# The end of an audio-tower kernel: the last token group transposed by VectorE and SBUF moves instead of TensorE, routed by sums, its expert weights gathered in three pieces

## The chip, the core and the metric

The kernel runs on one core of a Trainium2 chip. The metric is the device time of one execution in microseconds (us); of several executions the median is taken. All data is float32.

## The reference

64 clips of 80,000 samples are cut into 157 frames of 512 samples, and each frame is turned into 512 DCT coefficients. Then comes one layer of a causal phase-memory attention with a gate, and after it a feed-forward part with one expert for each clip:

```python
h = _L0_tok_ref(x)                         # (64, 157, 512)
h = h + _L0_attn_ref(_layernorm(h), ...)
y = _layernorm(h)
scores = softmax(mean(y, axis=1) @ Wg + bg)       # (64, 16)
idx = argmax(scores); gate = scores[idx]
h = h + gate * (y @ We[idx] + be[idx])            # We: (16, 512, 512)
```

The change concerns this last part for the last four clips: the mean over a clip's tokens, the choice of its expert, the fetch of that expert's 512x512 matrix, and the product of the 157 tokens with it.

## The kernel before, in words

The 64 clips go in 16 groups (`NG`) of four (`GB`). A clip's 157 tokens are padded to 160 and cut into five tiles of 32 tokens; a tile of 128 partitions holds 32 tokens of each of the four clips. Tile number 4 (`TAIL`) has only 29 real tokens for each clip. The tiles are worked in the order `ORDER` = 4, 0, 1, 2, 3.

The order of all instructions on every engine is the order of the calls in the text of the kernel (`manual_schedule`); each engine takes its own in order. SyncE, ScalarE and GpSimd also issue DMAs, in the same order as their other work; a DMA that reuses a semaphore waits for the earlier one on it. PSUM is a pool of four buffers (`psum`) of two banks, given out in turn; a buffer is free again when its last reader is done.

The stages of neighbouring groups overlap. While group g goes through values, gate and attention, group g-1 is routed, its expert weights are gathered, and its expert products are done at the end of g's stages. So after the attention of the last group (g = 15) the five expert products of group 14 and the whole expert part of group 15 remain. That end is the place of the change. In the numbering of the kernel before it runs as follows.

- **Normalise.** `statistics2` (line 756) takes mean and variance of a tile on VectorE, the reciprocal deviation and the shift on GpSimd (`deviation`, `shifts`, lines 237 to 244). `normal2` (772) makes the normalised tile x2 (128 tokens x 512) on ScalarE (line 784), or, where `at_end` (768) says so, on VectorE (782) without the shift.
- **Turn.** The expert product needs x2 with features on the partitions. For groups 0 to 14 `turn_blocks` (787) transposes 32x32 blocks on VectorE (line 793), and `move_blocks` (795) brings the blocks to their partitions with 16 DMAs within SBUF (line 805). For the last group `turn_x2` (809) uses four TensorE transposes for each tile (line 816) and a copy out of PSUM (817).
- **Route.** Groups 0 to 14 sum the turned tokens on VectorE (`xsum`, 820) and multiply by the router's weights there (`route_own`, lines 837 to 841), then one matmul (848) adds over partitions and spreads the result. The last group multiplies all tokens by the router's weights on TensorE (`route_tokens`, line 858), sums on VectorE (`route_sum`, 865) and spreads by a matmul (`route_spread`, 871). `pick` (878 to 891) then finds logits, maximum and expert number on VectorE.
- **Fetch.** `fetch` (893) computes row numbers on VectorE (903) and gathers each clip's matrix by an indirect DMA of GpSimd (907). The last group's four matrices go to buffers no longer used (`wv`, `wg`, `spare`, `t_v`), in two pieces each; between the two pieces `biases` (called at 905) runs `pick_gate` (the softmax value, with one exponential on ScalarE, line 920) and `bias`, which gathers the experts' bias rows (937). The bias buffer `be` is single.
- **Product.** `expert_chunk` (949) is four matmuls in four 32-column groups of TensorE, one for each clip, for one of four parts c of the 512 features (line 953); four chunks make a tile. `add_bias` (944, line 947) adds the gated bias to the residual, `expert_out` (961, line 964) adds the gated product, both on VectorE, and stores the tile (line 971). A tile of the last two groups goes out by SyncE, ScalarE or GpSimd as lines 968 to 970 say.

In the trace a float32 matmul shows as two records, so a chunk of four matmuls has eight. The end, word for word:

```python
    expert(g - 1, ORDER[0])
    normal2(g, 1)
    turn_x2(g, TAIL)
    ...
    add_bias(g - 1, ORDER[1])
    expert(g - 1, ORDER[1], routes)
    ...
    for c in range(2):
        for n, ps in zip(order, banks):
            expert_chunk(g, n, c, ps)
```

`routes` puts `route_tokens` ahead of chunk 1 of that tile, and the spread, the pick and the fetch ahead of chunk 2. The last group's five tiles first do chunks 0 and 1 of all tiles, which need the first pieces of the weights alone, and then chunks 2 and 3 tile by tile.

Of the kernel before, what the change touches and what calls it, by code (L numbers as in the profile page):

```python
# [14 lines left out]
F32 = mybir.dt.float32  # L15
# [38 lines left out]
def audio_tower(ctx: ExitStack, tc: tile.TileContext, a, out):  # L54
# [118 lines left out]
    rowbase = load("rowbase", [P, 3])  # L173

    wv = const.tile([P, C, D], F32, name="wv", tag="wv")
    wg = const.tile([P, C, D], F32, name="wg", tag="wg")
# [543 lines left out]
    def output_product(g, i):  # L720

        s = S[g]
        ps = product(g, i, fac_o)
        (r11, r12), (r21, r22) = ([r[:, :, n : n + H] for n in (0, H)] for r in s["res2"])
        last = g + 1 == NG
        more = lambda to, x: add(to, to, x)
        if i == 1:
            s["u"] = [p2.tile([P, 2, H], F32, tag="u", name="u") for _ in range(2)]
            nc.scalar.copy(s["u"][0], ps)
        first, second = s["u"]  # L730
        if i == 2:
            add(r11, ps, r11)
            if last:
                add_bias(g - 1, ORDER[0])
        elif i == 6:
            add(first, ps, first)
            more(r12, first)
            more(r21, first)
        elif i == 7:
            add(second, ps, first)  # L740
            more(r22, second)
        elif i == 5:
            add(r22, ps, r22)
        elif i == 3:
            add(r12, ps, r12)
        elif i == 4:
            add(r21, ps, r21)
            for of in ((2,), (3,)) if last else ((2, 3),):
                statistics2(g, of)

    def output_tail(g):
        s = S[g]
# [14 lines left out]

    def at_end(g, n):

        return g + 1 == NG and n in (3, 0, 1)  # L770

    def normal2(g, n):
        s = S[g]
# [13 lines left out]
    def turn_blocks(g, n):  # L787

        s = S[g]
        if n == TAIL:  # L790
            s["blocks2"] = p1.tile([P, C * GB, LP], F32, tag="gT", name="turned2")
        to = s["blocks2"].rearrange("p (q c) t -> p c q t", c=C)[..., Q * n : Q * (n + 1)]
        nc.vector.transpose(to, s.pop(("x2", n)).rearrange("p (c q t) -> p c q t", c=C, q=GB))

    def move_blocks(g):

# [12 lines left out]
    def turn_x2(g, n, copy=nc.scalar.copy):  # L809
        s = S[g]  # L810
        if n == TAIL:
            x = p1.tile([P, C, 2 * HN], F32, tag="xT", name="x2T_last", bufs=2)
            s["x2T"] = x.rearrange("p c (b t) -> p c b t", b=GB)
        x, tr = s.pop(("x2", n)), bank()
        for c in range(C):
            nc.tensor.transpose(tr[:, c * P : (c + 1) * P], x[:, c * P : (c + 1) * P], ident)
        copy(s["x2T"][:, :, :, Q * n : Q * (n + 1)], tr.rearrange("p (c b t) -> p c b t", c=C, b=GB))


    def xsum(g, lo, hi):  # L820

# [29 lines left out]
    def route_tokens(g):  # L851

        s = S[g]
        s["each"] = ps = bank()[:, :L]
        rwg = s.pop("rwg")
        for c in range(C):
            for b in range(GB):
                nc.tensor.matmul(
                    ps[Q * b : Q * (b + 1), :], rwg[:, c, :], s["x2T"][:, c, b, :L], start=(c == 0), stop=(c == C - 1)
                )  # L860

    def route_sum(g):
        s = S[g]
        s["tot"] = tot = p2.tile([P, 1], F32, tag="tot", name="tot")
        nc.vector.tensor_reduce(tot, s.pop("each"), AX.X, ALU.add)

    def route_spread(g):

        s = S[g]
        ps = bank()[:, :P]  # L870
        nc.tensor.matmul(ps, s.pop("tot").to_broadcast([P, P]), ident, start=True, stop=True)
        s["all"] = ps.rearrange("p (b e) -> p b e", b=GB)[:, :, :E], 1.0 / L

    t = lambda name, shape, dt=F32: p2.tile(shape, dt, tag=name, name=name)
    wide = [P, GB, E]
# [14 lines left out]
        s["rev"] = rev = t("rev", [P, GB])  # L890
        nc.vector.tensor_reduce(rev, score, AX.X, ALU.max)

    def fetch(g, rooms=(), parts=1, between=lambda: None):
        s = S[g]
        ws = [
            rooms[b] if b < len(rooms) else p1.tile([P, C * D], F32, tag="we", name="we", bufs=GB) for b in range(GB)
        ]
        n = C * D // parts
        of = a["we"].rearrange("r (k n) -> (r k) n", k=parts)
        for k in range(parts):  # L900
            rows = t("rows", [P, GB], I32)
            base = rowbase[:, parts + k - 1 : parts + k]
            nc.vector.tensor_scalar(rows, s["rev"], float(-P * parts), base, ALU.mult, ALU.add)  # L903
            if k:
                between()
            for b in range(GB):
                nc.gpsimd.indirect_dma_start(  # L907
                    out=ws[b][:, n * k : n * (k + 1)],
                    out_offset=None,
                    in_=of,  # L910
                    in_offset=bass.IndirectOffsetOnAxis(ap=rows[:, b : b + 1], axis=0),
                )
        s["ws"] = [w.rearrange("p (c o) -> p c o", c=C) for w in ws]

# [46 lines left out]
    def expert_out(g, n, ps):  # L961
        s = S[g]
        o, at = s["res"][n], Q * BLOCK[n]
        nc.vector.scalar_tensor_tensor(o, ps, s["gate"], o, ALU.mult, ALU.add)
        for i in range(GB):

            for lo, hi in ((0, Q),) if n < TAIL else ((0, Q // 2), (Q // 2, LT)):
                queue = nc.sync if g + 1 < NG or i % 2 == 0 else nc.scalar
                if g + 2 == NG and n in ORDER[1:4]:
                    queue = nc.gpsimd  # L970
                queue.dma_start(out=out[GB * g + i, at + lo : at + hi, :], in_=o[Q * i + lo : Q * i + hi, :])

    def expert(g, n, between=lambda c: None):
# [287 lines left out]
        attention(g)  # L1261

    g = NG - 1
    expert(g - 1, ORDER[0])
    normal2(g, 1)
    turn_x2(g, TAIL)
    turn_x2(g, 2)
    turn_x2(g, 3, nc.vector.tensor_copy)
    turn_x2(g, 0)
    turn_x2(g, 1, nc.vector.tensor_copy)  # L1270


# [4 lines left out]
    def biases():  # L1277
        pick_gate(g)
        bias(g)

    def routes(c):
        if c == 1:
            route_tokens(g)
            route_sum(g)
        elif c == 2:
            route_spread(g)
            pick(g)
            fetch(g, [*flat, all_v.rearrange("p i c o -> p (i c o)")], 2, biases)

    add_bias(g - 1, ORDER[1])  # L1290
    expert(g - 1, ORDER[1], routes)
    add_bias(g - 1, ORDER[2])
    expert(g - 1, ORDER[2])
    for n in (3, 4):
        add_bias(g - 1, ORDER[n])
        expert(g - 1, ORDER[n])

    last = psum()
    banks = [last[:, 0, :], *(bank() for _ in range(3)), last[:, 1, :]]
# [6 lines left out]
    for n, ps in zip(order, banks):  # L1306
        for c in range(2, C):
            expert_chunk(g, n, c, ps)
        expert_out(g, n, ps)
# [3 lines left out]
def _constants():  # L1313
# [15 lines left out]
    def trig(half, n, turn):  # L1329
# [10 lines left out]
    setsel = np.tile(np.repeat(np.eye(SETS), PLANES, axis=0), (2, 1))  # L1340
    f = lambda x: np.ascontiguousarray(x, dtype=np.float32)

    sums = [x.sum(axis=0) for x in tables]
    table_sums = np.concatenate([sums[0] + sums[1], sums[2] + sums[3], sums[4], sums[5]]) / -D
    return {
# [11 lines left out]
        "rowbase": f(np.stack([n * (np.arange(P) + P * E) + k for n, k in ((1, 0), (2, 0), (2, 1))], axis=1)),  # L1357
    }


# [61 lines left out]
```

## Time and profile before

| what | value |
|---|---|
| median of 3 runs (lowest, highest) | 1303.95 us (1301.6, 1304.43) |
| the profiled execution's own time | 1301.98 us |
| its span (first to last instruction or landing) | 1300.0 us |
| TensorE busy | 1293.2 us, 99% |
| VectorE busy | 1023.6 us, 79% |
| GpSimd busy | 592.7 us, 46% |
| ScalarE busy | 431.9 us, 33% |
| granted TensorE clock, mean | 0.999 |
| DMA moved | 144.46 MB, mean 111 GB/s |

How to read it: durations of the profile are those of the one profiled execution. TensorE's matmuls overlap, so its busy time is not a measure of how well it is used, and a gap in it shows only as a fall below 100%. The queries used in what follows can be limited to a window of time, given in us from the start of the span.

### The profile page before, as it was taken

To read this page: it belongs to the slowest core of one execution; us is meant where nothing else is said; L and a number is where in the kernel's file an instruction comes from. 1 tells how busy PE (TensorE), PEld (TensorE's weight loads), DVE (VectorE), ACT (ScalarE), POOL (GpSimd) and SP (SyncE) were. 2 spreads that over 40 slices of the span, in tenths; PEclk is the share of its full clock that TensorE was granted. 3 is DMA by queue.
4 is the path that set the end of the run, shared out by engine and by line. 5 is a ranking of instruction groups with operands and counts; after the bars stand their busy time and mean duration, and the time that the engine had idled before them with its cause. 6 is when DMAs were issued, how large, how long until landed. Compare 5 with 4: busy or idle time off the path is not lost.

```text
span 1300.0 us, 26072 instructions
## 1 busy us (share of the span) xinstructions
PE 1293.2 (99%) x10152; PEld 864.7 (67%) x10152; DVE 1023.6 (79%) x2056; ACT 431.9 (33%) x768; POOL 592.7 (46%) x781
## 2 busy tenths in 40 slices
PE   9999999999999999999999999999999999999998
PEld 5677666676666767666676666766666676666762
DVE  6888787878877887788878878788778877888583
ACT  2525334142432324334242331424323243342410
POOL 2356445344553446435444453446434454354424
PEclk9999999999999999999999999999999999999999
DMA  7015224252442425323252342424323262241506
GB/s 242 1 52 178 76 61 173 61 171 75 114 147 54 152 75 177 93 57 146 80 183 76 77 174 49 166 75 131 128 64 145 75 193 77 58 154 36 181 9 210
DMA packets 60578, 144.46 MB, mean 111 GB/s; under 512 B 14136, under 2 KB 31432, under 8 KB 52520
## 3 DMA queue, kind: packets, MB, share of 16 engines
q1 hardware_dynamic: 45620, 62.68, 17.6%
q0 software_dynamic: 14336, 79.47, 17.2%
q8 instruction: 81, 1.33, 0.4%
q10 hardware_dynamic: 500, 0.64, 0.2%
q14 instruction: 41, 0.34, 0.1%
HBM read 102.47 MB, written 20.62 MB: 95 GB/s over the span
## 4 chain that ended last, share of the span: by engine, by line
PE 97%; DMA 1%; POOL 1%; issue 0%; SPq 0%; DVE 0%; POOLq 0%
PE mm L445 29%; PE mm L953 20%; PE mm L658 17%; PE mm L250 10%; PE mm L705 9%; PE mm L270 3%; PE mm L272 3%; PE mm L601 3%; PE mm L637 1%; PE mm L689 1%; DMA tables<-in_table_sums 1%; DMA t_v<-in_we,rows 1%; PE mm L201 0%; PE mm L219 0%; PE mm L684 0%
## 5 line engine op out<-in xcount | busy, mean ns | idle before, releaser
L953 PE MATMUL mm<-we,x2T 128*32 128x512 f32 x2400 | 263.8, 593 | 0.0
L953 PEld LDWEIGHTS mm<-we,x2T 128*32 128x32 f32 x2400 | 75.0, 110 | 165.6 <-issue 165.5
L237 POOL TENSOR_SCALAR rstd<-mv 128x2 f32<-128x2 f32 (+1 forms) x50 | 11.7, 235 | 241.0 <-DVE mv L233 240.9
L516 POOL TENSOR_TENSOR v<-v,bv 128x512 f32<-128x512 f32 (+1 forms) x45 | 72.7, 1632 | 101.2 <-ACT v L465 101.2
L705 PE MATMUL mm<-att,v 32*128 32x320 f32 (+3 forms) x2048 | 113.2, 357 | 0.0
L705 PEld LDWEIGHTS mm<-att,v 32*128 32x128 f32 x2048 | 94.6, 185 | 22.0 <-issue 12.6
L784 ACT ACTIVATE x<-res,shift,rstd 128x512 f32<-128x512 f32 x61 | 46.4, 807 | 172.7 <-POOL shift L244 171.9
L327 POOL TENSOR_TENSOR res<-res,bo 128x512 f32<-128x512 f32 x64 | 95.7, 1514 | 13.1 <-ACT res L323 13.0
L100 DVE TENSOR_TENSOR gT<-mm,gT 128x320 f32<-128x320 f32 (+3 forms) x128 | 71.2, 566 | 31.7 <-PE mm L658 28.7
L712 DVE TENSOR_TENSOR gT<-mm,gT 128x320 f32<-128x320 f32 x128 | 59.5, 485 | 42.4 <-PE mm L705 42.3
L237 POOL TENSOR_SCALAR dev<-mv 128x5 f32<-128x5 f32 (+1 forms) x20 | 4.9, 244 | 188.7 <-DVE mv L233 188.1
L232 DVE BATCH_NORM_STATS2 st<-res 128x6 f32<-128x512 f32 x128 | 87.9, 686 | 3.3
L445 PE MATMUL mm<-t_o,sum 128*128 128x256 f32 x384 | 85.5, 379 | 0.0
L445 PE MATMUL mm<-t_v,sum 128*128 128x256 f32 x360 | 80.1, 379 | 0.0
L445 PEld LDWEIGHTS mm<-t_o,sum 128*128 128x128 f32 x384 | 73.0, 190 | 9.9
L676 ACT ACTIVATE gT<-gT,hbg 128x320 f32<-128x320 f32 (+1 forms) x90 | 45.6, 554 | 100.1 <-DVE gT L100 100.1
L323 ACT ACTIVATE res<-res,shift,more 128x512 f32<-128x512 f32 x64 | 46.9, 803 | 87.2 <-POOL more L313 87.2
L907 POOL DMA_INDIRECT we<-in_we,rows x60 | 59.9, 998 | 34.4 <-DVE rows L903 20.4
L445 PEld LDWEIGHTS mm<-t_v,sum 128*128 128x128 f32 x360 | 68.4, 190 | 9.3
L250 PE MATMUL mm<-wv,xT 128*128 128x512 f32 x160 | 71.8, 592 | 0.0
L658 PE MATMUL mm<-sum,wg 128*128 128x320 f32 (+1 forms) x240 | 69.2, 431 | 0.0
L658 PE MATMUL mm<-xT,wg 128*128 128x317 f32 x240 | 68.9, 430 | 0.0
(223 smaller groups left out, 2832.3 us busy)
## 6 DMA issues: line engine op xcount, KB each, us to landing
xT<-in_frames SPq DMA_DIRECT2D x32, 640.0 KB
out<-res SPq DMA_DIRECT2D x236, 64.0 KB
x2T<-turned SPq DMA_DIRECT2D x150, 80.0 KB
x2T<-turned POOLq DMA_DIRECT2D x90, 80.0 KB, 1.9
scale<-row SPq DMA_DIRECT2D x15, 320.0 KB
out<-res_t SPq DMA_DIRECT2D x62, 32.0 KB
out<-res_t SPq DMA_DIRECT2D x62, 26.0 KB
wg<-in_wg SPq DMA_DIRECT2D x1, 1024.0 KB
```

What stands on the lines that cost most here:

```text
L100: add = lambda *x: nc.vector.tensor_tensor(*x, ALU.add)
L232: nc.vector.bn_stats(st, h)
L250: nc.tensor.matmul(ps, tile_of(x[:, c], n), w[:, c, :], start=(c == 0), stop=(c == C - 1))
L323: nc.scalar.activation(s["res"][n], s["res"][n], AF.Identity, bias=shift, scale=more)
L327: nc.gpsimd.tensor_tensor(r, r, bo, ALU.add)
L445: nc.tensor.matmul(ps[:, b, :], lhs[:, c, P * b : P * (b + 1)], w[:, c, :], start=(first and c == 0), stop=(c == 1), skip_group_check=not ...
L516: nc.gpsimd.tensor_tensor(v, v, by, ALU.add)
L658: nc.tensor.matmul(ps[:, o, :width], w[:, c, o * P : (o + 1) * P], rhs[:, c, :width], start=(first and c == 0), stop=(c == 1), skip_group_ ...
L705: nc.tensor.matmul(to, s["v", n][q, c * P : (c + 1) * P], by, start=(n == 3), stop=(n == TAIL))
L712: nc.vector.tensor_tensor(th, r[:, :, 0], th, ALU.mult)
L907: nc.gpsimd.indirect_dma_start(out=ws[b][:, n * k : n * (k + 1)], out_offset=None, in_=of, in_offset=bass.IndirectOffsetOnAxis(ap=rows[:, ...
L953: nc.tensor.matmul(ps[Q * i : Q * (i + 1), :], s["x2T"][:, c, i, Q * n : Q * (n + 1)], s["ws"][i][:, c, :], start=(c == 0), stop=(c == C - 1),
```

## The change

In words:

- The last group's x2 tiles are transposed by `turn_blocks` on VectorE, and `move_last` moves the blocks by 16 DMAs of 32 partitions x 640 elements, eight issued by SyncE and eight by ScalarE. `turn_x2` goes.
- `route_tokens` now reads x2 before it is turned: for each tile, each of four feature parts and each of four 32-column groups one matmul with 32 stationary columns and a moving operand of four columns, which hold ones for the tokens of each clip. That is 80 matmuls. `route_features` multiplies the sums by the router's weights and reduces, on VectorE; `route_spread` is four matmuls with 64 moving columns.
- The sums stand between the second and third chunk of group 14's second expert tile, the spread, the pick and the fetch ahead of the first chunk of its third tile. The outputs of group 14's first two tiles are written after the fetch is issued; its bias adds come in one go.
- `fetch` for the last group has three pieces of each matrix: a quarter, a quarter, and a half. All row numbers are computed first. The gather of the bias rows stands after all of them.
- The last group's bias adds come one at a time, each ahead of the tile's output.
- Statistics of tiles 2 and 3 of the last group are taken together as for other groups, and only tile 1 is normalised on VectorE.
- The stores of three tiles of group 14 (12 DMAs) go by ScalarE instead of GpSimd. The constant `rowbase` grows from 3 to 12 columns.

The diff, cut to its core:

```diff
-            for of in ((2,), (3,)) if last else ((2, 3),):
-                statistics2(g, of)
+            statistics2(g, (2, 3))
...
-        return g + 1 == NG and n in (3, 0, 1)
+        return g + 1 == NG and n == 1
...
+    def move_last(g):
+        s = S[g]
+        x = p1.tile([P, GB, C, LP], F32, tag="xT", name="x2T_last", bufs=2)
+        of = s["blocks2"].rearrange("p (q c) t -> p q c t", c=C)
+        for b in range(GB):
+            for q in range(GB):
+                queue = nc.sync if q % 2 == 0 else nc.scalar
+                queue.dma_start(out=x[Q * q : Q * (q + 1), b], in_=of[Q * b : Q * (b + 1), q])
+        s["x2T"] = x.rearrange("p b c t -> p c b t")
...
+    def route_tokens(g, of):
+        s = S[g]
+        if "sums2" not in s:
+            s["sums2"] = psum()
+        for n in of:
+            x = s["x2", n]
+            at = 4 + GB * (n == TAIL)
+            for c in range(C):
+                for q in range(GB):
+                    nc.tensor.matmul(
+                        s["sums2"][Q * q : Q * (q + 1), 0, GB * c : GB * (c + 1)],
+                        x[:, c * P + Q * q : c * P + Q * (q + 1)],
+                        rowbase[:, at : at + GB],
+                        start=(n == TAIL and c == 0),
+                        stop=(n == 1),
+                        skip_group_check=True,
+                    )
+
+    def route_features(g):
+        s = S[g]
+        total = s["sums2"][:, 0, : C * GB].rearrange("p (c b) -> p b c", c=C)
+        by = s.pop("rwg")[:, :, :E].rearrange("p c e -> p e c")
+        part = p2.tile([P, GB, E, C], F32, tag="u", name="part")
+        over = [P, GB, E, C]
+        nc.vector.tensor_tensor(part, by.unsqueeze(1).to_broadcast(over), total.unsqueeze(2).to_broadcast(over), ALU.mult)
+        own = p2.tile([P, GB * E], F32, tag="own", name="own")
+        nc.vector.tensor_reduce(own, part.rearrange("p b e c -> p (b e) c"), AX.X, ALU.add)
+        s["own"] = own
 
     def route_spread(g):
         s = S[g]
-        ps = bank()[:, :P]
-        nc.tensor.matmul(ps, s.pop("tot").to_broadcast([P, P]), ident, start=True, stop=True)
+        own, ps = s.pop("own"), s.pop("sums2")[:, 1, : GB * E]
+        for q in range(GB):
+            rows = slice(Q * q, Q * (q + 1))
+            nc.tensor.matmul(ps[rows], mean[:, rows], own, start=True, stop=True)
...
+    def fetch(g, rooms=()):
+        s = S[g]
+        ws = rooms or [p1.tile([P, C * D], F32, tag="we", name="we", bufs=GB) for b in range(GB)]
+        pieces = ((4, 0), (4, 1), (2, 1)) if rooms else ((1, 0),)
...
+        for i, (parts, k) in enumerate(pieces):
+            base = rowbase[:, i + len(rooms) // GB : i + len(rooms) // GB + 1]
+            nc.vector.tensor_scalar(rows[:, i], s["rev"], float(-P * parts), base, ALU.mult, ALU.add)
+        for i, (parts, k) in enumerate(pieces):
+            n = C * D // parts
+            of = a["we"].rearrange("r (k n) -> (r k) n", k=parts)
             for b in range(GB):
                 nc.gpsimd.indirect_dma_start(
                     out=ws[b][:, n * k : n * (k + 1)],
...
                 if g + 2 == NG and n in ORDER[1:4]:
-                    queue = nc.gpsimd
+                    queue = nc.scalar
...
     g = NG - 1
-    expert(g - 1, ORDER[0])
+    first = psum()[:, 0, :]
+    for c in range(C):
+        expert_chunk(g - 1, ORDER[0], c, first)
+    for n in (TAIL, 2, 3):
+        turn_blocks(g, n)
     normal2(g, 1)
-    turn_x2(g, TAIL)
-    turn_x2(g, 2)
-    turn_x2(g, 3, nc.vector.tensor_copy)
-    turn_x2(g, 0)
-    turn_x2(g, 1, nc.vector.tensor_copy)
+    turn_blocks(g, 0)
...
+    def sums(c):
+        if c == 2:
+            route_tokens(g, (TAIL, 2, 3, 0, 1))
+            route_features(g)
+            turn_blocks(g, 1)
+            move_last(g)
 
     def routes(c):
-        if c == 1:
-            route_tokens(g)
-            route_sum(g)
-        elif c == 2:
+        if c == 0:
             route_spread(g)
             pick(g)
-            fetch(g, [*flat, all_v.rearrange("p i c o -> p (i c o)")], 2, biases)
+            fetch(g, [*flat, all_v.rearrange("p i c o -> p (i c o)")])
+            expert_out(g - 1, ORDER[0], first)
+            pick_gate(g)
+            add_bias(g - 1, ORDER[1])
+            expert_out(g - 1, ORDER[1], second)
+            for n in ORDER[2:]:
+                add_bias(g - 1, n)
+            bias(g)
 
+    second = psum()[:, 0, :]
+    for c in range(C):
+        sums(c)
+        expert_chunk(g - 1, ORDER[1], c, second)
+    expert(g - 1, ORDER[2], routes)
+    for n in ORDER[3:]:
+        expert(g - 1, n)
...
-    for n in order:
-        add_bias(g, n)
     for n, ps in zip(order, banks):
+        add_bias(g, n)
         for c in range(2, C):
             expert_chunk(g, n, c, ps)
         expert_out(g, n, ps)
```

More of the change, by code (lines that the diff above doesn't have):

```diff
@@ L172, in audio_tower @@
     revexp = load("revexp", [P, GB, E])
-    rowbase = load("rowbase", [P, 3])
+    rowbase = load("rowbase", [P, 4 + 2 * GB])
     wv = const.tile([P, C, D], F32, name="wv", tag="wv")
@@ L792, in turn_blocks @@
         to = s["blocks2"].rearrange("p (q c) t -> p c q t", c=C)[..., Q * n : Q * (n + 1)]
-        nc.vector.transpose(to, s.pop(("x2", n)).rearrange("p (c q t) -> p c q t", c=C, q=GB))
+        nc.vector.transpose(to, s["x2", n].rearrange("p (c q t) -> p c q t", c=C, q=GB))
+    def move_last(g):
[7 more added lines that the diff above has]
+        s["x2T"] = x.rearrange("p b c t -> p c b t")
     def move_blocks(g):
@@ L807, in move_blocks @@
         yield
[L809 to L817, printed above, removed]
     def xsum(g, lo, hi):
@@ L849, in route_all @@
         s["all"] = ps.rearrange("p (b e) -> p b e", b=GB), D / L
-    def route_tokens(g):
+    def route_tokens(g, of):
         s = S[g]
[L854 to L862, printed above, removed]
-        s = S[g]
-        s["tot"] = tot = p2.tile([P, 1], F32, tag="tot", name="tot")
-        nc.vector.tensor_reduce(tot, s.pop("each"), AX.X, ALU.add)
+        if "sums2" not in s:
[13 more added lines that the diff above has]
+                    )
@@ L867, in route_spread @@
     def route_spread(g):
         s = S[g]
-        ps = bank()[:, :P]
-        nc.tensor.matmul(ps, s.pop("tot").to_broadcast([P, P]), ident, start=True, stop=True)
-        s["all"] = ps.rearrange("p (b e) -> p b e", b=GB)[:, :, :E], 1.0 / L
+        own, ps = s.pop("own"), s.pop("sums2")[:, 1, : GB * E]
+        for q in range(GB):
+            rows = slice(Q * q, Q * (q + 1))
+            nc.tensor.matmul(ps[rows], mean[:, rows], own, start=True, stop=True)
+        s["all"] = ps.rearrange("p (b e) -> p b e", b=GB), D / L
@@ L891, in pick @@
         nc.vector.tensor_reduce(rev, score, AX.X, ALU.max)
-    def fetch(g, rooms=(), parts=1, between=lambda: None):
+    def fetch(g, rooms=()):
         s = S[g]
[L895 to L905, printed above, removed]
+        ws = rooms or [p1.tile([P, C * D], F32, tag="we", name="we", bufs=GB) for b in range(GB)]
+        pieces = ((4, 0), (4, 1), (2, 1)) if rooms else ((1, 0),)
+        rows = [
+            p2.tile([P, len(pieces), GB], I32, tag="each", name="rows")
+            if rooms
+            else t("rows", [P, GB], I32).unsqueeze(1)
+        ][0]
+        for i, (parts, k) in enumerate(pieces):
[4 more added lines that the diff above has]
+            of = a["we"].rearrange("r (k n) -> (r k) n", k=parts)
             for b in range(GB):
@@ L910, in fetch @@
                     in_=of,
-                    in_offset=bass.IndirectOffsetOnAxis(ap=rows[:, b : b + 1], axis=0),
+                    in_offset=bass.IndirectOffsetOnAxis(ap=rows[:, i, b : b + 1], axis=0),
                 )
@@ L1275, in audio_tower @@
     flat[2] = flat[2][:, : C * D]
-    def biases():
-        pick_gate(g)
-        bias(g)
+    def sums(c):
[4 more added lines that the diff above has]
+            move_last(g)
     def routes(c):
-        if c == 1:
-            route_tokens(g)
-            route_sum(g)
-        elif c == 2:
+        if c == 0:
             route_spread(g)
             pick(g)
-            fetch(g, [*flat, all_v.rearrange("p i c o -> p (i c o)")], 2, biases)
[L1290 to L1296, printed above, removed]
+            fetch(g, [*flat, all_v.rearrange("p i c o -> p (i c o)")])
[13 more added lines that the diff above has]
+        expert(g - 1, n)
     last = psum()
@@ L1303, in audio_tower @@
             expert_chunk(g, n, c, ps)
-    for n in order:
+    for n, ps in zip(order, banks):
         add_bias(g, n)
-    for n, ps in zip(order, banks):
         for c in range(2, C):
@@ L1341, in _constants @@
     f = lambda x: np.ascontiguousarray(x, dtype=np.float32)
+    bases = np.stack([n * (np.arange(P) + P * E) + k for n, k in ((1, 0), (4, 0), (4, 1), (2, 1))], axis=1)
+    member = np.kron(np.eye(GB), np.ones((Q, 1)))
     sums = [x.sum(axis=0) for x in tables]
@@ L1356, in _constants @@
         "revexp": f(np.tile(E - np.arange(E), (P, GB, 1))),
-        "rowbase": f(np.stack([n * (np.arange(P) + P * E) + k for n, k in ((1, 0), (2, 0), (2, 1))], axis=1)),
+        "rowbase": f(np.concatenate([bases, member, member * (np.arange(P)[:, None] % Q < LT)], axis=1)),
     }
```

## The prediction

> **What bounds the kernel now.** The page says TensorE (PE) is busy for 99% of the span, so I looked for the one stretch where it isn't: the last 46 us. The chain of waits, read from 1254 us on, shows what that stretch is made of (columns: start, duration, what ran or what was waited for).
>
> ```profile
> 1254.26 3.57 PE mm L953 x32
> 1257.83 2.40 PE mm L816 x20
> 1260.23 0.99 PE mm L953 x8
> 1261.22 1.11 PE mm L858 x32
> 1262.33 0.86 PE mm L953 x8
> 1263.19 0.42 PE mm L871 x2
> 1263.61 1.90 PE mm L953 x16
> ...
> 1265.95 1.08 POOL wv L907
> ...
> 1271.18 2.67 issue
> ...
> 1279.37 7.29 DMA t_v<-in_we,rows
> 1286.66 0.04 issue
> 1286.71 8.79 PE mm L953 x74
> ```
>
> After 1265.95 the chain leaves PE. It runs through GpSimd's (POOL's) nine gathers, and the landing of the last (t_v, second half) lets PE finish. From 1286.71 everything is fixed: 8.8 us of matmuls, one VectorE (DVE) pass of 0.75, the last stores until 1300.0. So **the end is the landing of the last gathered weights plus 13.3 us**; what PE saves earlier counts only through that. The wait timeline of GpSimd says why the gathers take so long:
>
> ```profile
> 1274.08 0.95 POOL L937 DMA_INDIRECT be<-in_be,expi  x1 [2.89 <-DVE res L947]
> 1275.33 0.94 POOL L907 DMA_INDIRECT wv<-in_we,rows  x1 [0.30 <-issue]
> ```
>
> The bias gather stood 2.9 us in the middle of the queue, waiting for the old bias's last reader. In three windows (share of the 16 DMA engines, then GB/s, are the last two columns):
>
> ```profile
> 1260.00:1268.00 8.00, 8.00 (x97) 3.17 (x98) 5.75 (x24) 0.60 (x2) 1.75 (x2) 1.00 0.18 34
> 1268.00:1278.00 10.00, 10.00 (x99) 3.52 (x91) 4.35 (x7) 0.00 (x0) 5.58 (x7) 1.00 0.75 244
> 1278.00:1286.00 8.00, 7.73 (x67) 3.52 (x59) 2.91 (x5) 0.00 (x0) 5.49 (x9) 1.00 0.94 323
> ```
>
> First half: the DMA engines have a quarter free. Second half: they are full. PE ran out of work at about 1284.4 (ten chunks of four matmuls, 0.86 us each, from 1275.6), so the stall is about 2.3 us. That is all the change can win at the landing alone.
>
> [...] The new route sums are 160 records of 4 columns[...]. The nearest row of the trace, also 32-column tiles in four column groups, is L684: one window has 8 records busy for 0.27 us in all, 0.206 us each, so starts lie (0.27 - 0.206) / 7 = 9 ns apart. I go by the trace, 1.4 us[...]. [...]at a share of 0.94 SyncE's stores and GpSimd's gathers split 323 GB/s. I go by it: stores handed from GpSimd to ScalarE (ACT) are not free, they move ahead of the last weights.
>
> **The change, part by part.** All sums are against the profiled execution: span 1300.0, its own time 1301.98, which is 2.0 below the median of 1303.95; I carry the difference over to the median.
>
> PE, 1254.26 to the last group's first matmul. Removed: 2.40 (transposes) + 1.11 (routing) + 0.42 (spread) = 3.93. Added: sums 1.4[...], spread in four tiles 0.2 (8 records at 9 ns plus one latency; bounds 0.1 and 0.4). So 20 chunks x 0.86 + 1.6 = 18.8, and the last group could start at 1273.1 instead of 1275.6: 2.3 to 2.5 us saved on PE, not yet on the end.
>
> The route. Two chunks after the sums cover DVE's product and reduction (0.43 and 0.42 by the rows L837 and L839 of the earlier groups, 128x256, all from SBUF; here one operand is in PSUM, taken as the same). Sums end at 1254.26 + 6 x 0.86 + 1.4 = 1260.8, the chunks at 1262.5, the spread lands at 1262.9. Before, logits began at 1263.65, so 0.75 earlier. The pick is unchanged; the first gather goes from 1265.95 to 1265.2. It needs only the first of three row computations, the other two (0.2 each) run beside its issue.
>
> DVE. Added: five transposes at 0.69 (L793) = 3.5, product and reduction 0.85, one more row computation 0.2. Removed: two copies of 0.69, two normalisations of 0.53 (to ScalarE, 0.81 each), one reduction 0.32. Net about +1.8, at nothing: four transposes lie beside PE's first six chunks, the fifth beside the two chunks after the sums; DVE sat 7.7 us idle before 1288.65. If that cover went, the first gather would slip by as much. Statistics of tiles 2 and 3 taken together add 0.8 to x2's tile 2 (1255.8 to 1256.6); PE needs it only from 1259.4.
>
> The move. Sixteen DMAs of 80 KB, eight each on SyncE and ScalarE. SyncE issued ten of them in 6.21 us for group 15, so eight take 5 us: 1262.6 to 1267.6, landing near 1270 to 1272; PE needs them at 1273. Queued behind: on SyncE the eight stores of the old tail (nobody waits); on ScalarE the exponential. VectorE waits for that at about 1268, and behind it stand the old group's bias adds and outputs. The output of the second tile frees the PSUM bank for the fifth at 1269.6; it comes near 1270.4. Up to 1 us of PE, hidden only because PE waits for weights anyway.
>
> The gathers. Nine become thirteen: two quarters and a half of four matrices, then the bias. Issue spacing is 1.24 to 1.56, mean 1.30, and the bias row (a quarter's size) issues no faster (0.95 against 0.94), so it is per gather, not per byte. Last weights: 1265.2 + 11 x 1.30 = 1279.5, against 1279.37 now. **The 2.9 us wait and the bias's own slot are gone, and four more gathers fill exactly that hole.** Landing took 6.0 after issue with free engines and 7.3 with full ones. In the new kernel more is moved ahead of it: what is left of the moves once gathers flow (0.6 MB), the old tail's stores (0.23), and twelve stores of 64 KB, of which about five went by then before (net 0.45), less the bias (0.26). About 1.0 MB at 323 GB/s is 3.2 us; the windows above left 2.5 + 0.5 us of DMA idle to take it. I add 0.4 for what doesn't fit: 1279.5 + 7.3 + 0.4 = 1287.2, **0.5 us later than now**. Bounds: 5.5 after issue (wv's first, idle engines) gives 1285.0, -1.7; all 3.2 us added gives 1290.0, +3.3.
>
> The quarters. Last first quarter: issued 1269.1, landing 3.4 to 6.0 later, 1272.5 to 1275.1, wanted at 1273.1. Second quarters: issued by 1274.3, 1277.7 to 1281, wanted 4.3 us after the first. Stalls of up to 2 us each, inside the slack: PE then comes to the halves at 1282 to 1286, still before 1287.2. So PE's 2.4 us become waiting.
>
> The bias behind it all: issued at 1280.8, landing about 1 us behind t_v, 1288.3. PE ends the tail tile at 1287.2 + 1.7 = 1288.9. Five bias adds and five outputs, queued behind this wait, take 5 x 1.49 = 7.5 on DVE and must end by 1296.8: it costs only if it lands after 1289.3, then one for one. The wider row table costs nothing: it loads at the start, a thousand us ahead of its use.
>
> Sum: -2.4 on PE (hidden), -0.75 at the first gather, +0.85 by the last issue, +0.4 at landing = **+0.5**: span 1300.5, 1304.5 against the median.
>
> **Rivals.** (a) The light case: small pieces find free engines, t_v lands at 1285.0: -1.7, 1302.3. For it: a quarter of the DMA time was free. Against: ScalarE now stores in that time. A gain over 2.6 us needs a landing before 1284.1, 4.6 us after issue; only the bias gather (3.4) did that. (b) The slower side: moves, stores and gathers share the full engines from 1266 on, the quarters back up, and t_v lands at 1290: +3.3, 1307.3. It decides from a landing at 1289.3. For it: SBUF moves run at 131 GB/s for half of the engines' time, costlier per byte than gathers. (c) The change doesn't do what it says: [...]PE saves nothing, [...]1307.1.
>
> **Numbers.** Forecast 55% (own range 1303.0 to 1306.5), (a) 19%, (b) 17%, (c) 9%. About 0.2%, 2.6 us, is what a measurement of this kernel can tell from no change; the three runs shown span 2.8. Faster: a third of (a), 7%. Slower: most of (b), half of (c) and a sliver of the forecast, 23%. Same: 70%. The range takes in (a) less half a us and (b) and (c) plus about 1 for the runs' own scatter: 1301.6 to 1308.3.
>
> **What would show it.** PE's first last-group matmul ready near 1273 but waiting for gathers; sums near 1.4 us; first gather at 1265.2, the last near 1279.5; t_v landing at 1287.2; DMA share over 0.9 from 1268 on. I am wrong if PE never waits at the halves, if the chain ends in the bias adds, or if PE's longer waits lower its granted clock (it fell to half only after the last matmuls, near 1298).

## The result, and the profile after

The changed kernel takes 1312.73 us (median of 6 runs, 1312.1 to 1313.08), the kernel before in the same comparison 1301.82 (6 runs, 1301.45 to 1304.43): a ratio of 1.0077 [1.0067, 1.0088], 0.8% slower. The forecast was 1304.5, its range ended at 1308.3. The profiled execution's span is 1311.0 us, 11.0 more than before; line numbers are now those of the changed kernel (L971 the expert products, L860 the sums, L876 and L878 the route on VectorE, L887 the spread, L925 and L955 the gathers, L982 the outputs).

The chain of waits of the changed kernel from 1250 us on (start, duration, what ran):

```profile
1253.82 5.27 PE mm L971 x46
1259.09 1.32 PE mm L860 x91
...
1262.73 0.32 PE mm L887 x8
1263.05 8.47 PE mm L971 x68
1271.52 1.14 issue
1272.67 0.59 PE mm L971
1273.26 0.86 issue
1274.12 0.90 PE mm L971
1275.02 1.92 issue
...
1282.88 1.09 issue
1283.97 22.27 PE mm L971 x183
```

The forecast expected PE to come to an empty weight buffer. Here it stops before that, and not at a buffer: "issue" is time in which nothing that the profile shows was waited for. From 1271.5 to 1284 PE executes one matmul of group 14's fifth tile at a time, with a pause of 0.9 to 1.9 us after each, though its weights and tokens have long been in SBUF. Its windows, with the columns of the same view of before:

```profile
1260.00:1268.00 8.00, 7.45 (x125) 2.84 (x119) 4.74 (x19) 0.00 (x0) 2.07 (x2) 1.00 0.42 90
1268.00:1278.00 10.00, 6.03 (x27) 1.22 (x19) 4.85 (x11) 0.26 (x1) 7.69 (x8) 0.81 1.00 317
1278.00:1286.00 8.00, 4.05 (x11) 1.11 (x15) 0.75 (x1) 0.00 (x0) 2.83 (x3) 0.50 0.90 322
```

Read the counts, not the busy time: 27 and 11 matmul records where before had 99 and 67. (No record is missing here: the trace holds all 160 of group 14's five tiles, 32 a tile. The outputs of VectorE below show the delay without them.) The DMA engines are full (1.00, 0.90), as forecast, and the granted clock falls to 0.50.

GpSimd does what was forecast, to 0.2 us. Three lines of its timeline: the first gather, the last one of the weights, the bias, none of them waiting for anything but its own issue (the first for the row numbers):

```profile
1265.42 1.08 POOL L925 DMA_INDIRECT wv<-in_we,rows  x1 [6.58 <-DVE rows L920]
...
1279.47 0.94 POOL L925 DMA_INDIRECT t_v<-in_we,rows  x1 [0.30 <-issue]
1280.71 0.95 POOL L955 DMA_INDIRECT be<-in_be,expi  x1 [0.30 <-issue]
```

The last packet of the gathers ends at 1287.55. VectorE shows the damage best, since it runs one output after each tile that PE finishes. The outputs of group 14's fourth and fifth tile in its timeline (idle time before, and its releaser, in brackets):

```profile
1284.87 0.75 DVE L982 SCALAR_TENSOR_TENSOR res<-mm,gate,res 128x512 f32<-128x512 f32 x1 [10.87 <-remote]
1289.10 0.75 DVE L982 SCALAR_TENSOR_TENSOR res<-mm,gate,res 128x512 f32<-128x512 f32 x1 [3.48 <-PE mm L971]
```

PE hands over the fifth tile at 1289.07; twelve chunks of 0.86 us after the spread would have been near 1273.4. From 1289.07 PE's remaining 20 chunks (17.2 us) run without a wait to 1306.24, the span ends at 1311.0. So of 15.7 us lost, about 5 go into the forecast's slack (halves reached at 1282 instead of 1287), and 10.5 come out at the end.

### The profile page after: what moved, and what is told of

The parts are those of the page before. It is cut to its first block, busy times and chain, and to the rows that moved or that the text cites. A ratio compares the mean times of both kernels' runs of the same rounds, so it can differ in the third digit from the quotient of the medians.

```text
span 1311.0 us, 26331 instructions
## 1 busy us (share of the span) xinstructions
PE 1296.2 (99%) x10266; PEld 865.0 (66%) x10266; DVE 1025.6 (78%) x2059; ACT 431.3 (33%) x767; POOL 590.6 (45%) x773
## 4 chain that ended last, share of the span: by engine, by line
PE 98%; issue 1%; DMA 0%; DVE 0%; SPq 0%
PE mm L445 29%; PE mm L971 22%; PE mm L658 17%; PE mm L250 9%; PE mm L705 9%; PE mm L270 3%; PE mm L272 3%; PE mm L601 3%; PE mm L637 1%; PE mm L689 1%; PE mm L201 1%; PE mm L219 0%; DMA wv<-in_wv 0%; PE mm L684 0%; PE mm L847 0%
## 5 line engine op out<-in xcount | busy, mean ns | idle before, releaser
L971 PE MATMUL mm<-we,x2T 128*32 128x512 f32 x2400 | 271.4, 596 | 7.9 <-issue 7.9
L971 PEld LDWEIGHTS mm<-we,x2T 128*32 128x32 f32 x2400 | 77.0, 110 | 179.6 <-issue 179.3
L237 POOL TENSOR_SCALAR rstd<-mv 128x2 f32<-128x2 f32 (+1 forms) x49 | 11.4, 233 | 241.5 <-DVE mv L233 241.3
L925 POOL DMA_INDIRECT we<-in_we,rows x60 | 59.9, 999 | 34.3 <-DVE rows L920 20.3
```

Of the source, the lines that this page charges most:

```text
L925: nc.gpsimd.indirect_dma_start(out=ws[b][:, n * k : n * (k + 1)], out_offset=None, in_=of, in_offset=bass.IndirectOffsetOnAxis(ap=rows[:, ...
L971: nc.tensor.matmul(ps[Q * i : Q * (i + 1), :], s["x2T"][:, c, i, Q * n : Q * (n + 1)], s["ws"][i][:, c, :], start=(c == 0), stop=(c == C - 1),
```

## The experiments

**A measure for all runs.** From PE's semaphore signals to VectorE I read the time from the handing over of the spread to that of group 14's fifth tile, less what it takes at full speed (10.3 us where three tiles lie between, 12.2 in kernels of the form of before). This "extra" is 0 in before and 15.7 in the changed kernel. It comes from one profiled execution; the ratio beside it comes from the timed runs. It counts the lateness of a signal, and in three kernels the fifth tile's own matmul records end earlier than that: by them the extra is 0.5 in e8, 8.2 in e10 and 0.5 in e18. In e8 the sparse stretch then lies in the last group's first products (1274.4 to 1284.4). "Hardware queues" are the MB that the queues of SyncE and ScalarE carry from 1262 to 1284 us.

| kernel | us | ratio to before [95%] | extra, us | hardware queues, MB |
|---|---|---|---|---|
| before | 1301.82 | 1 | 0 | 0.33 |
| changed | 1312.73 | 1.0077 [1.0067, 1.0088] | 15.7 | 2.01 |
| e1 one sum | 1302.88 | 1.0010 [1.0003, 1.0017] | 0 | 2.23 |
| e2 burst alone | 1312.89 | 1.0076 [1.0059, 1.0093] | 0.3 | 0.24 |
| e3 bias last | 1300.98 | 0.9993 [0.9986, 1.0] | 0 | 0.39 |
| e4 no moves, turned by TensorE | 1307.95 | 1.0043 [1.0026, 1.0060] | 0 | 1.07 |
| e5 sums spread | 1312.71 | 1.0079 [1.0064, 1.0094] | 16.0 | 1.93 |
| e6 other boundary | 1315.04 | 1.0100 [1.0083, 1.0118] | 15.9 | 2.01 |
| e7 spread, two pieces | 1309.08 | 1.0047 [1.0034, 1.0061] | 9.7 | 1.75 |
| e8 no moves | 1307.11 | 1.0036 [1.0023, 1.0050] | 11.0 | 1.03 |
| e9 e7 with wide sums | 1312.76 | 1.0083 [1.0070, 1.0097] | 10.4 | 1.74 |
| e10 wide sums | 1315.69 | 1.0103 [1.0087, 1.0118] | 11.4 | 1.98 |
| e11 three sums | 1312.41 | 1.0071 [1.0056, 1.0087] | 14.6 | 2.03 |
| e12 first pieces only | 1299.56 | 0.9981 [0.9974, 0.9987] | 0.9 | 2.60 |
| e13 two sums, same experts | 1312.18 | 1.0077 [1.0061, 1.0092] | 15.9 | 2.07 |
| e14 stores by GpSimd | 1311.28 | 1.0071 [1.0055, 1.0086] | 13.4 | 1.55 |
| e15 e3, stores by ScalarE | 1303.14 | 1.0013 [1.0006, 1.0020] | 3.5 | 1.03 |
| e16 e7, stores by GpSimd | 1308.85 | 1.0049 [1.0035, 1.0063] | 7.0 | 1.59 |
| e17 e3 and idle moves | 1305.77 | 1.0024 [1.0017, 1.0032] | 5.8 | 1.37 |
| e18 e16 without moves | 1301.27 | 0.9990 [0.9983, 0.9997] | 3.9 | 0.35 |

**First: the burst.** My theory after the result was that the burst of the sums' 80 short matmuls (160 records; 320 instructions with their weight loads, in 1.32 us) brings on PE's slow stretch. The kernels were timed in batches, each beside runs of before, so kernels of different batches are compared by their ratios.

e1 cuts the sums to one tile of five:

```diff
-            route_tokens(g, (TAIL, 2, 3, 0, 1))
+            route_tokens(g, (1,))
```

> The changed kernel, but route_tokens sums only the tile of n = 1 (leaves out the sums of the four other tiles, so the last group's experts are chosen from a part of the tokens): 256 fewer instructions go through TensorE at the sums, and the moves, stores and gathers stay. Theory B (the burst of sums: 320 TensorE instructions in 1.3 us[...]): the stretch of one instruction each 0.7 or 1.4 us is gone, TensorE goes through group 14's fifth tile by 1274 and waits at the halves again, 1301 to 1305 us. Theory D (the moves, the stores and the quarters together keep the DMA engines full, and TensorE is slow while they are): the stretch stays, 1311 to 1313 us.

No stretch, 1302.88: it looked like proof. But other sums choose other experts: worked out from the inputs, the full sums give experts 14, 11, 8, 1 for the four clips, one tile's sums 0, 0, 0, 1. Two things were changed; e13 below takes them apart, and the burst theory did not survive it.

e2 puts 160 idle matmuls alone into before, ahead of its routing. (The expectation miscounts them: with the weight loads they are 640 instructions, not 320.)

```diff
+    def burst():
+        ps = bank()
+        for i in range(40):
+            for q in range(GB):
+                nc.tensor.matmul(
+                    ps[Q * q : Q * (q + 1), 4 * (i % 16) : 4 * (i % 16) + 4],
+                    mean[:, Q * q : Q * (q + 1)],
+                    mean[:, :GB],
...
+                )
```

> The kernel before, with 160 idle matmuls of 32 columns by 4 added ahead of the sums (their result is not used; nothing else changed, no moves, two pieces): 320 more TensorE instructions in about 1.4 us. Theory B: a stretch with one instruction each 0.7 or 1.4 us appears behind it, group 14's last tile ends late, 1307 to 1315 us. Theory D: no such stretch, 1.4 us of more work that TensorE's wait at the halves takes up, within 2 us of the kernel before (1301 to 1304).

1312.89, but by another mechanism. The chain of e2:

```profile
1263.49 1.37 PE mm L1285 x94
1264.86 2.49 issue
1267.35 1.89 PE mm L1285 x128
1269.23 2.13 issue
1271.37 0.55 PE mm L1285 x27
```

Two stops, each inside the burst, and none after it (extra 0.3): the routing is only late. The stops make 4.6 us of that; the burst's own matmuls and a granted clock of 0.50 from 1267.0 to 1277.24 add to it, so the spread ends at 1276.54 where before has 1263.61. The stops stand behind 20,417 and 20,673 recorded PE instructions, 256 apart. That is a real effect, told at the end, but not the sparse stretch, which has no long stop and lasts for 12 us.

e3 takes the one part of the change that cost nothing in the forecast, the bias gather behind the weights, into before:

```diff
-            fetch(g, [*flat, all_v.rearrange("p i c o -> p (i c o)")], 2, biases)
+            fetch(g, [*flat, all_v.rearrange("p i c o -> p (i c o)")], 2)
+            biases()
```

> The kernel before, with one edit: the bias's choice and gather are put behind the eight weight gathers instead of between the pieces, still on two pieces and TensorE's turn. Theories B and D alike: no slow stretch, no burst and no moves; the last weights land one issue earlier (1286.7 to about 1285.4), the end 1 us earlier, 1300 to 1301.8 us, unless group 14's outputs, which now wait longer for the bias, are late for the store or hold a bank: then 1302 to 1305.

1300.98. Its chain from the spread on shows PE without any wait, which no other kernel has:

```profile
1263.97 0.42 PE mm L871 x2
1264.39 30.12 PE mm L953 x272
```

e4 gives the changed kernel the turn by TensorE back, without moves (`turn_x2` as it was before):

```diff
-    for n in (TAIL, 2, 3):
-        turn_blocks(g, n)
...
-    turn_blocks(g, 0)
+    turn_x2(g, TAIL)
+    turn_x2(g, 2)
+    turn_x2(g, 3, nc.vector.tensor_copy)
+    turn_x2(g, 0)
+    turn_x2(g, 1, nc.vector.tensor_copy)
...
-            turn_blocks(g, 1)
-            move_last(g)
```

> The changed kernel with the last group's tokens turned by TensorE and copied out of PSUM as before (no VectorE turns of the last group, no moves within SBUF), and all else as changed: sums in 32-column tiles, three pieces, stores on ScalarE's queue. Theory B: the burst is there, so the slow stretch is too, 1308 to 1314 us. Theory D: the DMA engines have 16 transfers and 1.3 MB less to do in 1262 to 1273, the stretch is gone or under 3 us, 1301 to 1305 us.

No stretch; its 1307.95 seem to come from elsewhere: the transposes, a stop of 1.39 us within the sums (behind 20,417 instructions, as the first one of e2) and a first gather at 1269.74, 4.3 us later than in the changed kernel.

e5 spreads the sums, a tile at a time between the chunks; e6 leaves them and, since the first stop of e2 and that of e4 stand behind the same count, 20,417, shifts every later instruction by 188 places with idle matmuls at the start:

```diff
+        route_tokens(g, ((), (2,), (3, 0), (1,))[c])
...
+        for i in range(47):
+            q = slice(Q * (i % GB), Q * (i % GB) + Q)
+            nc.tensor.matmul(ps[q, :GB], ident[:, q], ident[:, :GB], start=True, stop=True)
```

> The changed kernel with its sums tile by tile between the chunks of group 14's first two expert tiles, in place of all five in one go: the same 320 TensorE instructions, over some 5 us in place of 1.3. Theory B ([...]the extra matmuls ahead of the kernel before stopped TensorE for 2.49 and 2.13 us exactly 256 instructions apart): no stop and no slow stretch, the last weights set the end as without four of the sums, 1301.5 to 1304 us. If the number of instructions or the moves beside it did it: 1308 to 1313 us.

> The changed kernel with 47 idle matmuls of 32 columns by 4 added to those that it begins with, 1 us after its start (nothing else changed): 188 TensorE instructions more[...]. Theory B: [...]no stop and no slow stretch, 1301.5 to 1304.5 us (0.2 to 0.5 us of idle matmuls included). If it is the burst itself[...]: 1310 to 1314 us.

Extra 16.0 and 15.9: neither the burst nor its place counts. **The burst theory falls here.**

**Second: the pieces, the number of sums, the moves.** e7 is e5 with two halves of each matrix, as before the change:

```diff
-        pieces = ((4, 0), (4, 1), (2, 1)) if rooms else ((1, 0),)
+        pieces = ((2, 0), (2, 1)) if rooms else ((1, 0),)
```

> The changed kernel with the sums spread as in the run before the last but in two pieces of weights instead of three, the bias behind the eight gathers. From the kernel before with its bias last, where TensorE did not wait at all in the last group: four gathers fewer (5 us) let the last weights land near 1284 instead of 1287, the first halves near 1275; TensorE then has 17.2 us of the last group from there, 4.6 to 6 us after it to the end: span 1297 to 1298.5, time 1299 to 1300.5 us. If the stores and moves hold the weights up: 1301 to 1304 us.

3.6 us less than e5, extra 9.7: the third piece makes it longer, but is not needed for it.

e8 leaves the moves out of the changed kernel:

```diff
-        x = p1.tile([P, GB, C, LP], F32, tag="xT", name="x2T_last", bufs=2)
...
+        s["x2T"] = S[g - 1]["x2T"]
```

> The changed kernel without the sixteen moves within SBUF (leaves them out: the last group's experts read group 14's turned tokens in their place); sums in one go, three pieces, stores as changed, so the routing and the gathers start as in the changed kernel. Theory B alone[...]: the stretch is there, 1309 to 1313 us. Theory B with D ([...]the long stretch only where the moves and the weights then fill the DMA engines too): [...]no long stretch, 1302 to 1305 us.

5.6 us less, half of what the change costs, but extra 11.0: the moves are not all of it. e9 and e10 make the sums with a quarter of the matmuls, one of 128 columns in place of four of 32, in e7 and in the changed kernel:

```diff
-                for q in range(GB):
-                    nc.tensor.matmul(
-                        s["sums2"][Q * q : Q * (q + 1), 0, GB * c : GB * (c + 1)],
-                        x[:, c * P + Q * q : c * P + Q * (q + 1)],
...
+                nc.tensor.matmul(
+                    s["sums2"][:, 0, GB * c : GB * (c + 1)],
+                    x[:, c * P : (c + 1) * P],
```

> As the run with spread sums and two pieces, but each sum as one matmul with 128 weight columns in place of four with 32: 80 TensorE instructions for all sums instead of 320[...]. Theory C (what slows TensorE later is the number of instructions that the sums put through it[...]): no slow stretch, the routing as early as spread or up to 1 us later, TensorE nearly without waits in the last group, 1299 to 1302 us. If something else of the changed kernel does it (the order of DVE's and ScalarE's work, the moves, the stores on ScalarE's queue): 1307 to 1310 us.

> The changed kernel with the sums as 20 matmuls of 128 weight columns in one go in place of 80 of 32 (80 instructions instead of 320[...]), all else as changed. Theory C: no slow stretch; routing and gathers 3 us later than changed, so 1304 to 1307 us. If the count does not matter: the stretch and the 3 us, 1313 to 1317 us.

Extra 10.4 and 11.4: still there, and both are slower in time (in e10 the granted clock was 0.50 already from 1262.46 to 1269.28, ahead of the spread). The number of PE's instructions isn't it either.

**Third: which experts, and how much is gathered.** e11 sums three tiles (its choice of experts is 0, 8, 2, 11), e13 two tiles chosen so that the experts are 14, 11, 8, 1 as with all five:

```diff
-            route_tokens(g, (TAIL, 2, 3, 0, 1))
+            route_tokens(g, (TAIL, 0, 1))
```

```diff
-            route_tokens(g, (TAIL, 2, 3, 0, 1))
+            route_tokens(g, (2, 1))
```

> The changed kernel with three of the five tiles summed (leaves out the sums of n = 2 and n = 3): 192 instructions in the burst. Theory C with a length that grows with the count (64 gave none, 320 gave 14 us): a stretch of 3 to 9 us, 1303 to 1308 us. A threshold: either none, 1302 to 1304 us, or all of it, 1311 to 1313 us.

> The changed kernel with only the tiles n = 2 and n = 1 summed (leaves out three; the last group's four experts come out as with all five, as worked out from the inputs): 128 instructions in the burst. Theory E (the sums do not matter; what is moved at the same time as the weights does, and the one-sum run was fast because three of its four gathers read the same expert): slow stretch, 1309 to 1313 us. If the sums matter: 1302 to 1304 us.

e12 gathers only the first quarter of each matrix:

```diff
-        for i, (parts, k) in enumerate(pieces):
+        for i, (parts, k) in enumerate(pieces[:1]):
```

> The changed kernel with only the first of the three pieces gathered (leaves out the eight later weight gathers; the last group's experts use the first quarter of the rows for all four chunks): the burst, the moves and the stores stay, 3.1 MB less is read between 1271 and 1287. Theory C with D (the count slows TensorE only while the DMA engines are full): the stretch is gone or under 4 us, TensorE runs through, 1296 to 1301 us, no weights being waited for. Theory C without D: the stretch stays, 1308 to 1313 us.

The window 1268 to 1278 of the three kernels e1, e13 and e12, in this order:

```profile
1268.00:1278.00 10.00, 10.00 (x93) 4.10 (x85) 6.17 (x13) 0.26 (x1) 7.56 (x9) 1.00 0.93 310
```

```profile
1268.00:1278.00 10.00, 5.41 (x21) 0.95 (x12) 4.85 (x11) 0.26 (x1) 7.56 (x9) 0.81 0.95 313
```

```profile
1268.00:1278.00 10.00, 9.75 (x76) 2.97 (x72) 5.65 (x13) 0.26 (x1) 3.38 (x4) 1.00 0.80 223
```

e11 has nearly the whole stretch (14.6) with other experts, four different ones. e13 sums two tiles instead of five and has all of it (21 matmul records): so e1's cure was not the shorter sums alone. e1 and e13 carry nearly the same share and rate (0.93 and 0.95, 310 and 313 GB/s), and e1's PE is untouched (93 records): **full DMA engines alone don't slow PE**. e12 carries more on the hardware queues than any other kernel (2.60 MB) and has almost nothing: without the later gathers the moves and stores do no harm.

**Fourth: moves and stores, each put into before and taken out again.** e14 gives the changed kernel's middle stores back to GpSimd; e15 gives those of e3 to ScalarE:

```diff
-                    queue = nc.scalar
+                    queue = nc.gpsimd
```

> The changed kernel with the stores of group 14's middle tiles back on GpSimd's queue, behind the gathers (one word). Theory S (the stores that ScalarE now issues while the weights come in, beside the moves, are what TensorE's stretch comes with): no stretch, 1302 to 1305 us. If the moves alone do it: 1310 to 1313 us. If moves and stores each do a part (without the moves it was 1307): 1305 to 1309 us.

> The kernel before with its bias last and the stores of group 14's middle tiles on ScalarE's queue instead of GpSimd's: no moves, no new sums, two pieces. Theory S: the stretch appears here too, 1305 to 1312 us. If the moves are needed: no stretch, 1300 to 1302 us.

e16 is e7 with these stores on GpSimd, e18 is e16 without moves (the edit of e8):

> The changed kernel with spread sums, two pieces, the bias last, and the stores of group 14's middle tiles on GpSimd's queue. Theory S: no stretch; first halves near 1276, TensorE through the last group from there, 1299 to 1301.5 us, at or below the kernel before with its bias last (1301). If the moves do it: 1306 to 1310 us.

> The two-piece run with spread sums and the stores on GpSimd's queue, without the sixteen moves (leaves them out: the last group's experts read group 14's turned tokens in their place). Theory M: nothing but GpSimd's gathers and SyncE's eight tail stores is under way, no stretch or one under 2 us, TensorE through the last group from about 1275.5: 1298 to 1300.5 us. If something else of the change holds TensorE up: 1304 to 1309 us, as with the moves.

e17 adds 16 idle moves to e3, of the changed kernel's size and on its queues; nothing reads them:

```diff
+    def idle_moves():
+        x = p1.tile([P, GB, C, LP], F32, tag="gT", name="idle")
+        of = S[g - 1]["x2T"].rearrange("p c b t -> p b c t")
+        for b in range(GB):
+            for q in range(GB):
+                queue = nc.sync if q % 2 == 0 else nc.scalar
+                queue.dma_start(out=x[Q * q : Q * (q + 1), b], in_=of[Q * b : Q * (b + 1), q])
```

> The kernel before with its bias last and, beside the last group's routing, sixteen moves within SBUF of the same shape and on the same two queues as in the changed kernel, into a tile that nobody reads; no sums of the new kind, no VectorE turns. Theory M (transfers on SyncE's and ScalarE's queues beside GpSimd's gathers are what TensorE slows under, whatever asked for them): a slow stretch in group 14's last tiles, 1305 to 1312 us. If the moves only do it together with the rest of the change: 1301 to 1303 us.

e17 is the cleanest of all: e3's chain above had no wait; the same chain with the idle moves:

```profile
1263.71 7.00 PE mm L953 x64
1270.71 0.12 issue
1270.83 1.06 PE mm L953 x4
1271.89 0.37 issue
...
1276.51 0.81 issue
...
1278.05 20.86 PE mm L953 x191
```

PE loses its stride at 1270.7 and gets it back at 1278, with the same "issue" pauses as the changed kernel, and no instruction of PE was added. By the ratios e17 is 0.31% above e3, 4 us; e15 is 0.20% above it, 2.6 us. The way out of the changed kernel's form agrees: from e16 to e18 the ratio falls by 0.59%, 7.7 us. Part of this is the clock. Three of e16's five executions had a mean granted clock of 0.996 or 0.997 and took about 1309; the two with 0.999 took 1304.91 and 1305.91, and all of e18's had 0.999 or more. Against those two the moves are 4 to 5 us, close to e17. The window 1268 to 1278 of e16 (the execution of 1304.91), and of e18:

```profile
1268.00:1278.00 10.00, 7.28 (x40) 1.53 (x32) 4.85 (x11) 0.26 (x1) 7.63 (x10) 1.00 0.96 292
```

```profile
1268.00:1278.00 10.00, 9.36 (x79) 2.51 (x72) 6.25 (x18) 0.26 (x1) 7.87 (x8) 1.00 0.81 264
```

With the moves 40 matmul records, without them 79. The stores give no such pair: taken out of the changed kernel (e14, 1.0071 against 1.0077) or of e7 (e16, 1.0049 against 1.0047) they change nothing that is clear of the scatter.

**What is shown, and what stays open.** Shown: moves that SyncE and ScalarE issue within SBUF slow PE when they run beside GpSimd's full set of weight gathers, with e1 as the one exception. They are worth 4 us put into before, and 5.6 (e8) and 7.7 (e18, with the clock's part) taken out. The stores cost 2.6 us put in, and nothing measurable taken out; three pieces cost 3.6 more than two. These parts depend on each other: without the moves the changed kernel still has a stretch. Not shown is the path by which a transfer holds PE. Four facts belong to it:

- The matmuls that come late wait for no semaphore, and their own signals are late as well: the last matmul record of group 14's fourth tile is at 1269.33, its signal at 1284.84, where 0.62 us is usual.
- The trace itself has holes there: of 740 four-byte semaphore updates that the DMA engines sent from 1262 to 1290 it holds 195 as arrived; in before 422 of 422, in e1 821 of 836, in e8 185 of 580, in e17 536 of 700. In the eleven kernels counted so, the missing share goes with the extra: at most 2% in before, e1, e3 and e4 (extra 0), 18 to 30% in e12, e15, e17 and e18 (0.9 to 5.8), 68 to 79% in the changed kernel, e8 and e13 (11.0 to 15.9). Some of the missing signals did arrive: VectorE's own have no record from 1265.56 to 1285.63, and instructions of VectorE that wait for them run in that time. Why the rest are missing no run here shows, and since all runs here were recorded, none tells whether recording has a part in PE's pauses: that is the rival left open.
- e1, with as much traffic as the changed kernel, has no stretch. Its three clips with the same expert read the same rows of HBM; this choice of experts was not tried with all sums.
- e4 and e8 both lack the moves, and only e8 has a stretch. In e4 gathers start 4.3 us later, so fewer lie beside the stores (2.19 MB by GpSimd's queue up to 1284, 3.63 in e8). That fits, but was not tried alone. e18's remaining 3.9 us are mostly a late signal (0.5 by its matmul records); why it is late is open.

**The best version** is e3: 1300.98 us, at most 0.14% faster than before, with an interval that reaches 1.0. (e12 and e18 leave part of the computation out.) No version that has the moves and gathers everything beats before.

## Why the prediction was wrong, point by point

- **PE's own work up to the spread: right.** The sums took 1.32 us in the chain (forecast 1.4). Their 160 records start between 1258.92 and 1260.27, 8.5 ns apart (34 ns within one of the four column groups), as the forecast had read from L684 (9 ns). Rival (c) assumed longer sums, which no trace had shown; it is refuted.
- **The route and the gathers: right.** The product with an operand in PSUM took 0.62 us instead of 0.43; logits at 1263.11, the first gather at 1265.42 (1265.2), the last of the weights at 1279.47 (1279.5), the bias at 1280.71 (1280.8); the last gathered packet at 1287.55 (t_v 1287.2). Thirteen gathers do fill the hole of the bias's wait.
- **The moves as transfers: 1 to 1.5 us slower than forecast.** Issued from 1262.2 to 1268.7 (6.1 us on SyncE, 6.5 on ScalarE; forecast 5), last packet at 1273.40 (1270 to 1272). The exponential behind them ran at 1268.75 (1268), the second tile's output at 1270.60 (1270.4). The wait of the fifth tile for that output's bank did not exist: its first matmul is at 1269.71, ahead of the output. DMA share 1.00 in the second window (over 0.9).
- **The failed step** is "Stalls of up to 2 us each, inside the slack: PE then comes to the halves at 1282 to 1286, still before 1287.2. So PE's 2.4 us become waiting." It let transfers touch PE only through a buffer not yet filled. In the runs they slowed PE at work that had all its data: PE finished group 14's last tile 15.7 us late, and came to the halves long after they had landed: "PE never waits at the halves", one of the forecast's own signs of being wrong, came true. The sum lacked this term altogether; only its excess over the slack, 10.5 us, shows in the time (span forecast 1300.5, measured 1311.0).
- **The granted clock**, which the forecast named as what would refute it, did fall to 0.50 from 1274.27 to 1287.92. It followed the pauses and added to them: rounds of a chunk between 1284.7 and 1288.5 took 0.78 to 0.86 us instead of 0.43 each, some 1.6 us of the 15.7.
- **Rival (b)** had the right traffic, though the engines were full only from 1270 on (share 0.59 from 1266 to 1268, 0.84 to 1270, then 1.04), and the wrong victim: it made t_v late (1290) and priced that at 3.3 us; t_v came at 1287.5 and PE was late instead.
- **Bias last** cost nothing, as forecast, and in before it gains at most 0.14% (e3): the end there was PE's own pace by then, not the last landing.

## What to carry to other kernels

A transfer had two prices here, when it landed and what it did to the engine that ran beside it (4 us in e17, where nothing reads it): before moving work from TensorE to SBUF-to-SBUF moves, put the bare moves, with nothing reading them, into the kernel as it is (e17) and look at the matmul counts of that window. Keep moves, and on weaker evidence stores (2.6 us in e15), on SyncE's and ScalarE's queues out of the time in which indirect gathers fill the DMA engines and TensorE must run at its pace. And when an experiment leaves out part of a sum that chooses data, compare choices too: e1 changed which experts were read and seemed to prove a theory that e13 refuted.

## What the runs showed of the hardware that was not expected

- **PE stopped within a row of short matmuls.** In e2, with 160 matmuls of 4 columns in a row, it stopped for 2.49 and 2.13 us exactly 256 instructions apart (128 matmul records and their weight loads) and started again at 1267.35 and 1271.37, 4.0 us for 256. The queue that the DMA view calls "instruction" moved 4 packets, 0.07 MB, from 1262 to 1284 there, and 1 packet, 0.02 MB, in that window of the changed kernel; that the stops were waits for these packets was not shown. The changed kernel, with 80 such matmuls in a row, shows no such stop within them; e4, with the same 80, has one of 1.39 us.
- **TensorE at one instruction (a matmul or a weight load) per 0.7 to 1.4 us with nothing to wait for**, beside DMA engines that are full at 317 GB/s (changed kernel), while nearly the same share and rate in e1 (0.93, 310 GB/s) leave it at full speed.
- **PE's clock fell after long pauses:** in the changed kernel 0.50 was granted from 1274.27 on, 2.8 us after the first pause, until 1287.92. In two kernels with shorter pauses it kept 1.00: in e8, whose pauses are 0.07 to 0.43 us and one of 1.51, and in e17 (0.11 to 0.81 us).
